# Softmax transpositions on the two row halves of TensorE, and layers 0 and 1 by groups of eight batches, in a four-layer graph network

## The chip, the cores and the metric

The kernel runs on one core of a Trainium2 chip. The metric is device time in microseconds (us), from the start of the program on the core to its end. The engines have short names in the profile: PE is TensorE's matmuls, PEld its weight loads, DVE is VectorE, ACT ScalarE, POOL GpSimd and SP SyncE. Each has its own instruction stream and runs it in order; semaphores tie the streams together. Matmuls write to PSUM, which has eight banks of 512 float32 per partition; all else lies in SBUF.

## The reference

Input x has 32 batches of 512 nodes with 64 features; adj is one 512 x 512 matrix. Four residual layers follow each other, all in float32. Each takes `h = relu(layernorm(x))` and adds a graph layer of h to x:

```python
# layer 0: x += h @ W_self + (adj @ h) @ W_nbr + bias
# layer 1: z = h; twice: z = relu((adj @ z) @ W_i); x += z
# layer 2 (GAT): Wh = h @ W.T; e = leaky_relu(e1[:, None] + e2[None, :], 0.2)
#                att = softmax(where(adj > 0, e, NEG)); x += elu(att @ Wh)
# layer 3: gat_layer(x, g, W, b):  h = x @ W;  s = (h @ h.T) * g;  s = where(s == 0, -1e16, s)
#                return softmax(s) @ h + b
#          8 heads of width 128, leaky_relu over them, one more gat_layer of width 64 on top,
#          leaky_relu, x += result
```

Layers 2 and 3 need a softmax over 512 x 512 scores: one for each batch in layer 2 and nine for each batch in layer 3 (eight heads and the output layer).

## The kernel before

The 512 nodes of a batch are split as partition p and column block c, with P = 128 partitions and C = 4 blocks. x stays in SBUF for the whole kernel as four tiles `xs[g]` of G = 8 batches each (L70). At the start seven DMAs on ACT's queue bring x (the first group two batches at a time), one on SP's brings the adjacency, and a chain of small ones on POOL's brings the weights. `ident`, the identity that transpositions need, is made on POOL ahead of these (L58). The adjacency is copied and transposed into `adj_p` and `adj_t` (L118 to L131).

Layers 0 and 1 (L187 to L327) work on pairs of batches, so that two batches of 64 features fill 128 columns. For a pair, layer 0 transposes h on PE (`pair_transpose`, L175), multiplies by the adjacency (`neighbours`, L237: four products accumulated in one bank, then an ACT copy), and projects (`project`, L247) with block-diagonal weights. Layer 1 has product, projection, relu, product, projection. The text of the kernel arranges this as one stream of slots: slot k holds layer 0 of pair k, layer 1 of pair k - 2, the end of layer 1 of pair k - 3, and the norms of the pairs k + 2 (layer 0), k - 1 (layer 1) and k - 4 (GAT), each taken over a pair alone (class `Norm`, L199). The tile framework orders each engine's instructions beforehand, with the order of the text as priority: where an instruction isn't ready by the framework's reckoning, one from later in the text may go ahead. It also puts in the semaphore waits and hands out the buffers of each pool.

Layers 2 and 3 (from L330) are a row of units, each a softmax for two things at once (k = 0, 1): 16 `Gat` units of two batches, 128 `Heads` units of two heads of one batch, and 16 `Out` units of two batches: 160 in all. A unit has four steps, and `run` (L684) lays the steps of neighbouring units over one another in slots. In slot k come, in the text: the current unit's scores for row block r (`flow_scores`, L543: two matmuls with 64 rows, one on each row half of TensorE, each into its own bank), the transposition of step j of the unit one unit and one slot back (`transpose`, L407), its reciprocal sums at j = 1 (`recips`), the values of the slot before (`values`, L420: two matmuls with 64 output columns each), the end of an earlier unit (`end`: normalising, then y_ps of Heads or the way back into x), the preparation of the next (`prep`: g_ps of Heads, gT_ps of Out), and last the softmax of row block r on DVE and ACT (`flow_rows` and `finish_rows`: s_att, t_att, negmax, then exp into `p_att`).

`transpose(j)` takes the probabilities `p_att`, which have rows n in partitions, and produces `pt_att` with columns m in partitions: for each k four transpositions of 128 x 128 into one bank `pt_ps`, followed by one ACT copy of 512 columns (L411 to L418). PSUM in these layers: `ps_s` two buffers of two banks for scores, `ps_m` three buffers of one bank shared by everything small (pt_ps, rec_ps, y_ps, g_ps, gT_ps, hx_ps and so on), `ps_v` one bank for av. gT_ps of an Out unit holds one of the three `ps_m` buffers for four slots.

`stats` (L140) takes mean and reciprocal deviation of a whole group of eight batches; before the change only layer 3's norms use it (from `Gat.end`, in two parts of 16 columns). `norm` (L163) subtracts the mean and applies relu and scale for a pair. Its statistics come from `gat_stats`, one entry for each pair.

Of the kernel before, what the change touches and what calls it, by code (L numbers as in the profile page):

```python
# [14 lines left out]
P = 128  # L15
# [7 lines left out]
def gnn_stack_kernel(  # L23
# [34 lines left out]
    ident = const.tile([P, P], F32, name="ident")  # L58
    make_identity(nc, ident)

# [8 lines left out]
    for g in range(NG):  # L69
        xg = xpool.tile([P, G, C, F], F32, name=f"x{g}")  # L70
        step = 2 if g == 0 else G
        for k in range(0, G, step):
            nc.scalar.dma_start(
                xg[:, k : k + step],
                x[g * G + k : g * G + k + step].rearrange("b (p c) f -> p b c f", c=C),
            )
        xs.append(xg)
# [36 lines left out]

    eps = const.tile([P, 1], F32, name="eps")
# [47 lines left out]
    def norm(pool, g, j, st):  # L163
        mean, rstd = (t[:, :, :, None].to_broadcast([P, 2, C, F]) for t in st)
        h = pool.tile([P, C, 2, F], F32, name="hn")
        hv = h.rearrange("p c k f -> p k c f")
        nc.vector.tensor_tensor(hv, xs[g][:, 2 * j : 2 * j + 2], mean, OP.subtract)
        for k in range(2):
            nc.vector.scalar_tensor_tensor(
                hv[:, k], hv[:, k], 0.0, rstd[:, k], op0=OP.max, op1=OP.mult  # L170
            )
        return h
# [11 lines left out]

    gat_stats = [None] * (B // 2)  # L187
    with (
        tc.tile_pool(name="ln_a", bufs=3) as lnp,
        tc.tile_pool(name="h_a", bufs=6) as hap,  # L190
# [4 lines left out]
        def pair_of(i):  # L195
            b = 2 * i
            return xs[b // G][:, b % G : b % G + 2]

        class Norm:  # L199


            def __init__(self, i):
                self.i = i

            def a(self):
                x4 = pair_of(self.i)
                self.mean = tiny.tile([P, 2, C], F32, name="mean2", bufs=B // 2 + 6)
                nc.vector.tensor_reduce(self.mean, x4, AX.X, OP.add)
                nc.vector.tensor_scalar(self.mean, self.mean, 1.0 / F, None, op0=OP.mult)
                self.h = hap.tile([P, C, 2, F], F32, name="hn")  # L210
                self.hv = self.h.rearrange("p c k f -> p k c f")
                nc.vector.tensor_tensor(
                    self.hv, x4, self.mean[:, :, :, None].to_broadcast([P, 2, C, F]),
                    OP.subtract,
                )
                self.sq = lnp.tile([P, 2, C, F], F32, name="sq")
                nc.scalar.activation(self.sq, self.hv, AF.Square)

            def b(self):
                var = tiny.tile([P, 2, C], F32, name="var2")  # L220
                nc.vector.tensor_reduce(var, self.sq, AX.X, OP.add)
                self.std = tiny.tile([P, 2, C], F32, name="std2")
                nc.scalar.activation(self.std, var, AF.Sqrt, bias=eps, scale=1.0 / F)

            def c(self):
                self.rstd = tiny.tile([P, 2, C], F32, name="rstd2", bufs=B // 2 + 6)
                nc.vector.reciprocal(self.rstd, self.std)

            def relu(self):
                for k in range(2):  # L230
                    nc.vector.scalar_tensor_tensor(
                        self.hv[:, k], self.hv[:, k], 0.0,
                        self.rstd[:, k, :, None].to_broadcast([P, C, F]),
# [38 lines left out]
        def norms(some):  # L272
            some = [n for n in some if n is not None]
            for n in some:
                n.a()
# [485 lines left out]
```

## Time and profile before

| | us |
|---|---|
| median of 3 runs | 2917.16 (2911.72 to 2918.14) |
| the profiled execution | 2918.14 |
| its span in the profile | 2916.4 |
| layers 0 and 1, last matmul of projection po1b | ends about 261.6 |
| ACT copies of pt_ps (L418), 1280 of them | 679.3 busy, 581 ns each |
| transpositions (L413), 5120 of them | 714.5 busy, 282 ns each |
| scores (L547), 2048 matmuls of Heads | 661.2 busy |
| values (L425), 2048 matmuls of Heads | 579.0 busy |

Busy time of an engine counts the stretches in which at least one of its instructions is under way, and groups of matmuls overlap, since each starts before the one before it has left the array. So for PE the distance from start to start says what an instruction costs, and the mean length of one (282 ns for a transposition) does not. A float32 product is two matmul instructions; a transposition is one. A line of the timeline gives start, length, engine, line of the kernel, operation, output and inputs, rows*columns of the array in use, shape, and how many instructions were merged. In the rows of groups the figures after the bar are busy us, mean ns of one, and idle time of the engine just before them with what ended it. In the table by stages each row ends with the granted TensorE clock (1.00 is full), the busy share of the DMA engines and GB/s.

### The profile page before, as it was taken

The numbers are of one execution on the slowest core, as the hardware profiler recorded it, in microseconds if no ns is written. First come the engines' busy times: TensorE is split into PE (matmuls) and PEld (weight loads), VectorE is DVE, ScalarE is ACT, GpSimd is POOL, SyncE is SP. The second block draws the span as 40 slices with busy tenths as digits, with TensorE's granted clock in tenths as the row PEclk, the third lists the DMA queues.
The fourth block names the chain that finished last, engine by engine and source line by source line (L and its number), as shares of the span: only waits on it lengthen the run. The fifth ranks groups of instructions, "written<-read, shape, count | busy, mean of one in ns | idle before, by whom it ended". The sixth has DMA issues, their size and how long they took to land.

```text
span 2916.4 us, 41809 instructions
## 1 busy us (share of the span) xinstructions
PE 2813.4 (96%) x15532; PEld 1380.0 (47%) x15532; DVE 2407.5 (83%) x4870; ACT 2049.0 (70%) x4687; POOL 52.7 (2%) x49
## 2 busy tenths in 40 slices
PE   7998887899999999999999999999999999999998
PEld 4555544444444444444444444444444444444443
DVE  6665889899798988888888888888888888888884
ACT  2333767677777778777777777777777777777775
POOL 3000000000000000000000000000000000000000
PEclk9998999899999999999999999999999999999999
DMA  3000000000000000000000000000000000000000
GB/s 86 1 1 1 1 1 1 1 1 1 1 5 4 1 4 1 4 1 5 1 4 1 4 1 4 1 5 1 4 1 5 1 5 1 4 1 4 1 4 4
DMA packets 9916, 13.10 MB, mean 4 GB/s; under 512 B 1016, under 2 KB 9376, under 8 KB 9584
## 3 DMA queue, kind: packets, MB, share of 16 engines
q1 hardware_dynamic: 4752, 5.24, 0.5%
q10 hardware_dynamic: 4208, 4.19, 0.5%
q8 instruction: 122, 2.00, 0.3%
q0 software_dynamic: 752, 0.99, 0.2%
q14 instruction: 82, 0.67, 0.1%
HBM read 6.23 MB, written 4.19 MB: 4 GB/s over the span
## 4 chain that ended last, share of the span: by engine, by line
PE 88%; DVE 6%; ACT 3%; issue 1%; POOL 1%; DMA 1%; POOLq 0%; DVEq 0%; ACTq 0%
PE av L425 20%; PE pt_ps L413 20%; PE s_ps L547 19%; PE rec_ps L436 6%; PE g_ps L591 5%; PE y_ps L619 4%; PE nt_ps L240 4%; PE gT_ps L642 3%; PE nt1b_ps L240 2%; ACT p_att L401 1%; DVE s_att L536 1%; PE po L251 1%; DVE t_att L397 1%; PE wh_ps L474 1%; DVE l_att L397 1%
## 5 line engine op out<-in xcount | busy, mean ns | idle before, releaser
L401 ACT ACTIVATE p_att<-t_att,negmax 128x512 f32<-128x512 f32 x1152 | 825.3, 717 | 466.3 <-DVE negmax L397 466.2
L536 DVE TENSOR_TENSOR s_att<-s_ps,adj_p 128x1024 f32<-128x1024 f32 x576 | 703.3, 1221 | 228.6 <-PE s_ps L547 228.6
L413 PEld LDWEIGHTS pt_ps<-ident,p_att 128*128 128x128 f32 x5120 | 554.8, 142 | 492.6 <-ACT p_att L401 187.5
L418 ACT COPY pt_att<-pt_ps 128x512 f32<-128x512 f32 x1280 | 679.3, 581 | 120.7 <-PE pt_ps L413 120.5
L397 DVE CUSTOM_DVE_ANT_0 t_att<-s_att,t_att 128x512 f32<-128x512 f32 x1152 | 752.3, 687 | 13.4
L413 PE MATMUL pt_ps<-ident,p_att 128*128 128x128 f32 x5120 | 714.5, 282 | 12.6 <-ACT p_att L401 7.5
L547 PE MATMUL s_ps<-hx,g 64*128 64x512 f32 x2048 | 661.2, 625 | 2.0 <-DVE s_att L536 2.0
L425 PE MATMUL av<-pt_att,hn 128*64 128x512 f32 x2048 | 579.0, 611 | 0.0
L540 DVE TENSOR_SCALAR t_att<-s_att 128x1024 f32<-128x1024 f32 x576 | 393.1, 683 | 24.3 <-ACT pt_att L418 0.5
L547 PEld LDWEIGHTS s_ps<-hx,g 64*128 64x128 f32 x2048 | 204.8, 185 | 311.3 <-issue 121.3
L401 ACT ACTIVATION_READ_ACCUMULATOR p_att<-t_att,negmax 128x1 f32 x1152 | 216.0, 187 | 0.0
L436 PE MATMUL rec_ps<-ident,rec 128*64 128x128 f32 x2560 | 186.6, 284 | 16.9 <-DVE rec L432 10.6
L436 PEld LDWEIGHTS rec_ps<-ident,rec 128*64 128x64 f32 x2560 | 144.4, 139 | 50.6 <-issue 26.5
L624 ACT ACTIVATE cat<-y_ps,bh 128x512 f32<-128x512 f32 x256 | 159.6, 672 | 4.4 <-PE y_ps L619 4.4
L425 PEld LDWEIGHTS av<-pt_att,hn 128*64 128x64 f32 x2048 | 115.6, 135 | 76.5 <-issue 76.2
L619 PE MATMUL y_ps<-o_att,wh_sb 64*128 64x512 f32 x512 | 145.8, 641 | 1.6 <-ACT pt_att L418 0.8
L591 PE MATMUL g_ps<-hx,m 64*128 64x512 f32 x256 | 144.6, 645 | 1.0 <-ACT pt_att L418 0.9
L642 PE MATMUL gT_ps<-cat,wo_sb 128*64 128x512 f32 x512 | 131.4, 595 | 0.0
L448 DVE TENSOR_TENSOR o_att<-av,recb 128x512 f32<-128x512 f32 x160 | 108.9, 681 | 21.8 <-PE av L425 20.6
L240 PE MATMUL nt_ps<-adj_t,hn 128*128 128x512 f32 x256 | 116.5, 598 | 0.0
L397 DVE DVE_READ_ACCUMULATOR2_ANT negmax<- 128x1 f32 x1280 | 104.7, 82 | 0.0
L444 ACT COPY recb<-rec_ps 128x512 f32<-128x512 f32 x160 | 93.9, 587 | 8.8 <-PE rec_ps L436 8.8
(131 smaller groups left out, 1930.4 us busy)
## 6 DMA issues: line engine op xcount, KB each, us to landing
out_dram<-x SPq DMA_DIRECT2D x32, 128.0 KB, 1.8
x<-in_x_dram ACTq DMA_DIRECT2D x3, 1024.0 KB, 13.7
x<-in_x_dram ACTq DMA_DIRECT2D x4, 256.0 KB, 7.9
adj_raw<-in_adj_dram SPq DMA_DIRECT2D x1, 1024.0 KB, 5.3
wh_sb<-in_L_gnn_Wh_dram POOLq DMA_DIRECT2D x2, 256.0 KB, 8.0
wo_sb<-in_L_gnn_W_out_dram POOLq DMA_DIRECT2D x1, 256.0 KB, 7.9
wl<-in_L_gnn_net_params_dram POOLq DMA_DIRECT2D x4, 16.0 KB, 7.0
bias_b<-in_L_gnn_bias_dram POOLq DMA_DIRECT2D x1, 32.0 KB, 7.6
```

The costliest lines, as they stand in the source:

```text
L240: nc.tensor.matmul(p, lhsT=lhs(k), rhs=adj_t[:, k, :], start=(k == 0), stop=(k == C - 1))
L397: nc.vector.tensor_tensor_reduce(out=ns[k], in0=s[k], in1=t[k], scale=-1.0, scalar=BIG, op0=OP.add, op1=OP.min, accum_out=self.negmax[:, k ...
L401: nc.scalar.activation(self.p[:, k, r, :], ns[k], AF.Exp, bias=self.negmax[:, k, r : r + 1], scale=-1.0, accum_out=self.sum[:, k, r : r + 1],)
L413: nc.tensor.transpose(ps[:, r * P : (r + 1) * P], self.p[:, k, r, j * P : (j + 1) * P], ident,)
L418: nc.scalar.copy(pt[:, k, :], ps)
L425: nc.tensor.matmul(self.av[halves(k), :], lhsT=self.v(k, j), rhs=pt[:, k, :], start=(j == 0), stop=(j == C - 1),)
L436: nc.tensor.matmul(ps[halves(k), r * P : (r + 1) * P], lhsT=rec[:, k, r : r + 1].to_broadcast([P, F]), rhs=ident, start=True, stop=True,)
L536: nc.vector.tensor_tensor(s, ps, adj_f[:, r, None, :].to_broadcast([P, 2, N]), OP.mult)
L540: nc.vector.tensor_scalar(t, s, 0.0, FLOW_NEG, op0=OP.is_equal, op1=OP.mult)
L547: nc.tensor.matmul(u.s_ps[:, k], lhsT=g[halves(k), r * P : (r + 1) * P], rhs=x[halves(k), :], start=True, stop=True,)
L591: nc.tensor.matmul(ps, lhsT=m2[rows, 2 * i : 2 * i + 2, :].rearrange("p h f -> p (h f)"), rhs=self.x[rows, :], start=True, stop=True,)
L619: nc.tensor.matmul(ps, lhsT=wh_sb[halves(k), h, :], rhs=self.o[halves(k), :], start=True, stop=True,)
```

## The change

There are three parts to it.

The softmax's transposition is done in halves. A 128 x 128 block of `p_att` becomes two inputs of 64 rows, one on each row half of the array, each with a 64 x 64 identity, and each gives 64 columns of the output. The first half's outputs of both k go to one bank, the second half's to another, and an ACT copy for each bank puts its 512 columns into `pt_att` in runs of 64. So both copies need all 16 transpositions, and the two banks are in use together.

```diff
         def transpose(self, j):
             pt = pbuf.tile([P, 2, N], F32, name="pt_att", bufs=3)
             self.pts = getattr(self, "pts", []) + [pt]
+            ps = [ps_m.tile([P, 2, C, F], F32, name="pt_ps", tag="m") for half in range(2)]
             for k in range(2):
-                ps = ps_m.tile([P, N], F32, name="pt_ps", tag="m")
                 for r in range(C):
-                    nc.tensor.transpose(
-                        ps[:, r * P : (r + 1) * P],
-                        self.p[:, k, r, j * P : (j + 1) * P],
-                        ident,
-                    )
-                nc.scalar.copy(pt[:, k, :], ps)
+                    for half in range(2):
+                        nc.tensor.transpose(
+                            ps[half][:, k, r],
+                            self.p[halves(half), k, r, j * P : (j + 1) * P],
+                            ident[halves(half), halves(half)],
+                        )
+            pth = pt.rearrange("p k (r half q) -> p k r half q", r=C, half=2)
+            for half in range(2):
+                nc.scalar.copy(pth[:, :, :, half, :], ps[half])
```

Layers 0 and 1 no longer run as a stream of slots. The class `Norm`, `norms`, `make`, `ends` and the loop over slots go; a loop over the four groups takes their place. In it, the group's statistics are taken at once, then all four norms, then the bias, then layer 0 of the four pairs, statistics again, layer 1 of each pair from norm to the final add, and statistics for the GAT. The transposed h of layer 0 is copied by DVE where ACT did it. `gat_stats` has one entry for each group.

```diff
+        for g in range(NG):
+            xg = xs[g]
+            st = stats(lambda shape: lnp.tile(shape, F32, name="sq"), G * C, g)
+            hs = [norm(hap, g, j, st) for j in range(G // 2)]
+            nc.gpsimd.tensor_tensor(
+                xg.rearrange("p b c f -> p (b c) f"),
+                xg.rearrange("p b c f -> p (b c) f"),
+                bias0_b[:, None, :].to_broadcast([P, G * C, F]),
+                OP.add,
+            )
+            for j, h in enumerate(hs):
                 ht = pair_transpose(
+                    ps_t, lambda n: wk.tile([P, N], F32, name=n), h, "ht0", nc.vector.tensor_copy
+                )
+                nt = neighbours(lambda k: h[:, k], "nt0")
+                po = project([(ht, ws2), (nt, wn2)], "po0")
+                for b in range(2):
+                    nc.vector.tensor_tensor(
+                        xg[:, 2 * j + b], xg[:, 2 * j + b], po[:, :, b, :], OP.add
+                    )
+            st = stats(lambda shape: lnp.tile(shape, F32, name="sq"), G * C, g)
+            for j in range(G // 2):
+                h = norm(hap, g, j, st)
+                nt = neighbours(lambda k: h[:, k], "nt1")
+                for i, w in enumerate(wl2):
+                    po = project([(nt, w)], f"po1_{i}")
+                    if i < len(wl2) - 1:
+                        z = wk.tile([P, C, F2], F32, name="z")
+                        nc.scalar.activation(z, po.rearrange("p c b f -> p c (b f)"), AF.Relu)
+                        nt = neighbours(lambda k: z[:, k, :], "nt1")
+                for b in range(2):
+                    nc.vector.scalar_tensor_tensor(
+                        xg[:, 2 * j + b], po[:, :, b, :], 0.0, xg[:, 2 * j + b],
+                        op0=OP.max, op1=OP.add,
+                    )
+            gat_stats.append(stats(lambda shape: lnp.tile(shape, F32, name="sq"), G * C, g))
```

The pools of these layers become `ln_a` with two buffers (three before, but of a quarter of the size) and `h_a` with `G // 2 + 2` = 6 as before. `norm` subtracts the mean batch by batch, two instructions of 256 elements where one of 512 stood, and takes its statistics as columns of the group's.

The start changes too: x comes in four DMAs of eight batches, even groups on ACT's queue and odd ones on SP's, and the identity is made after the weights' DMA issues on POOL.

```diff
-        step = 2 if g == 0 else G
-        for k in range(0, G, step):
-            nc.scalar.dma_start(
-                xg[:, k : k + step],
-                x[g * G + k : g * G + k + step].rearrange("b (p c) f -> p b c f", c=C),
-            )
+        eng = nc.scalar if g % 2 == 0 else nc.sync
+        eng.dma_start(xg, x[g * G : (g + 1) * G].rearrange("b (p c) f -> p b c f", c=C))
...
+    ident = const.tile([P, P], F32, name="ident")
+    make_identity(nc, ident)
     eps = const.tile([P, 1], F32, name="eps")
```

## The prediction

> **What bounds the kernel now.** I read the busy shares first, then the same by stage, then the order of TensorE's work inside one slot, then the rows of what changes. The page begins:
>
> ```profile
> span 2916.4 us, 41809 instructions
> ## 1 busy us (share of the span) xinstructions
> PE 2813.4 (96%) x15532; PEld 1380.0 (47%) x15532; DVE 2407.5 (83%) x4870; ACT 2049.0 (70%) x4687; POOL 52.7 (2%) x49
> ```
>
> TensorE (PE) fills 96%, VectorE (DVE) is not far behind. By stages (length, then busy us of PE, PEld, DVE, ACT, POOL, then the granted clock):
>
> ```profile
> 20.00:260.00 240.00, 231.78 (x953) 137.85 (x953) 146.44 (x336) 83.14 (x170) 18.89 (x15) 1.00 0.02 4
> 260.00:300.00 40.00, 30.42 (x124) 22.45 (x124) 29.33 (x73) 16.18 (x36) 0.00 (x0) 0.57 0.00 1
> 300.00:600.00 300.00, 250.17 (x1475) 142.89 (x1472) 267.53 (x595) 210.76 (x481) 13.70 (x6) 0.91 0.00 1
> 600.00:2800.00 2200.00, 2193.07 (x12406) 1026.93 (x12405) 1880.46 (x3701) 1661.65 (x3835) 4.57 (x2) 1.00 0.01 3
> ```
>
> Layers 0 and 1 run to about 262 us with PE never free from 27 us on. The GAT stage (to about 600) has PE at 83% and DVE at 89%: there PE is not the limit. Layer 3 (600 to 2800) is purely PE: 2193 of 2200, with DVE at 85.5% and ACT at 75.5%. In it one slot looks so in PE's timeline (start, length, operation):
>
> ```profile
> 1214.53 1.13 PE L619 MATMUL y_ps<-o_att,wh_sb 64*128 64x512 f32 x4
> 1215.49 1.02 PE L547 MATMUL s_ps<-hx,g 64*128 64x512 f32 x4
> 1216.45 1.09 PE L413 MATMUL pt_ps<-ident,p_att 128*128 128x128 f32 x8
> 1217.47 1.08 PE L425 MATMUL av<-pt_att,gV 128*64 128x512 f32 x4
> 1218.48 1.13 PE L547 MATMUL s_ps<-hx,g 64*128 64x512 f32 x4
> 1219.54 0.66 PE L413 MATMUL pt_ps<-ident,p_att 128*128 128x128 f32 x4
> ```
>
> From start to start: scores 0.96 after another 64-row operation (y_ps) but 1.06 after av, so a change of the array's form costs about 0.10 on entry; transpositions 1.02 for eight; values 1.01. The scores are four passes of 512 columns in 0.96, where the full-array neighbour products of layers 0 and 1 need 3.44 us for eight such passes in the chain of waits (0.43 each, so 1.72 for four): the two row halves do run side by side. A 64-row transposition exists once in this kernel, on one half:
>
> ```profile
> L354 PEld LDWEIGHTS whT_ps<-ident,wh_sb x8: 134/138/140, 262.5 to 262.9; 64*128 64x128 f32 x8
> L354 PE MATMUL whT_ps<-ident,wh_sb x8: 221/222/243, 262.5 to 262.9; 64*128 64x64 f32 x8
> ```
>
> The timeline gives this group 0.68 us in all; less one length of 0.22 that is 0.46 for seven steps, about 0.065 each, with loads included. A full one takes (1.02 - 0.10)/8 = 0.115.
>
> **The skill.** "TensorEngine Tiling (Array Packing)", Key Properties, says that a change of tiling mode drains TensorE and that tiles otherwise load and multiply independently; the 0.10 above and the side-by-side scores agree. Its Gotcha 1 asks for different PSUM banks for different row tiles, which the change observes; no transposition here shows it. "TensorE: Matmul & The Clock Gate", section on LDWEIGHTS, says that a load costs by columns, not rows: 138 ns with 64 rows against 140 with 128 here. Twice as many loads must therefore run in pairs to be free. Its Part 1 says that some 3.4 us of idleness halve the clock: the 0.57 at 260 to 300, where PE waits for the GAT's first rows, agrees.
>
> **Part 1, the transpositions.** Each slot issues 16 loads and 16 matmuls of 64 columns in place of 8 and 8 of 128. Side by side: 8 pairs x 0.065 = 0.52, plus 0.10 for leaving the form, 0.62 in place of 1.02. As the scores before it have the same 64-row form, the 0.10 between them goes too. Saved: 0.50 a slot. Layer 3 has 128 Heads and 16 Out units of 4 slots; the page has 5120 transpositions, 8 a slot, so 640 slots, 64 of them the GAT's. The window of 2200 us has 4380/8 = 548 slots: 274 us of PE time. What is late next is DVE: its 1880 us stay, and PE would need 2193 - 274 = 1919. Two engines with nearly the same load don't meet without loss: DVE's reciprocal waits 66.8 us for ACT's sums in this window even now, and 1880 + 67 = 1947 is a floor for DVE. The evacuations stay two ACT copies of 0.58, but both now wait for all 16 halves, where the first used to start after four transpositions; and both banks of the three in the shared PSUM pool must be free before the first transposition. Queued behind such a wait on PE are values, y_ps and the next scores, and DVE waits for those. One y_ps comes one values block (1.01) after the transpositions, while two copies need 0.2 + 1.16, so 0.3 to 0.5 us may be lost per unit, 137 units, 40 to 70 us if nothing absorbs it. I take 2020 for the window: a gain of 180. Best 1947 (253 gained), poorest about 2150 (50). Elsewhere (28 slots of layer 3, and the GAT, where DVE is the limit) 5. The copy's output in runs of 64 elements moves the same 512 elements; I cost it at nothing, 0.05 x 1280 = 64 us of ACT at worst, which has 24% free.
>
> **Part 2, layers 0 and 1.** PE's own work is the same: transpositions, three neighbour products and the projections of 16 pairs. What changes is what it waits for. A set of statistics is now taken for 8 batches at once: from the rows
>
> ```profile
> L154 POOL TENSOR_TENSOR sq<-sq 128x1024 f32<-128x1024 f32 x8 | 18.3, 2301 | 396.4 <-DVE sq L151 396.4
> L155 DVE TENSOR_REDUCE var<-sq 128x16 f32<-128x1024 f32 x8 | 9.8, 1220 | 9.7 <-POOL sq L154 9.7
> L151 DVE TENSOR_TENSOR sq<-x,mean 128x1024 f32<-128x1024 f32 x8 | 9.4, 1220 | 0.0
> L145 DVE TENSOR_REDUCE mean<-x 128x32 f32<-128x2048 f32 x4 | 9.1, 2280 | 0.0
> ```
>
> twice the length each where 1024 stands: 2.28 + 0.17 + 2.44 + 4.6 (GpSimd) + 2.44 + 0.32 + 0.34 = 12.6, some 13 with handovers. Between layers 0 and 1 of a group lie the adds (1.0), this 13 and a norm (4 x 0.415 = 1.7): 15.7 us. Between groups, serially, two statistics: 28.7. Within layer 1 a pair runs product, copy, projection, relu, product, copy, projection with three gaps of about 0.9, and the next norm may stand behind this pair's adds: 5.6 per pair; in layer 0 one gap, 0.9. With no overlap a group loses 15.7 + 28.7 + 22.4 + 3.6 = 70, four groups 280.
>
> But the engines' orders aren't the order of the text. The trace of before shows the builder filling waits with later work:
>
> ```profile
> 13.66 1.21 DVE L343 TENSOR_SCALAR neg<-adj_p 128x2048 f32<-128x2048 f32 x1
> ...
> 31.42 0.38 PE L251 MATMUL po<-ws,ht 128*128 128x128 f32 x2
> ...
> 31.64 0.60 PE L178 MATMUL ht_ps<-ident,hn 128*128 128x128 f32 x4
> ...
> 32.26 0.49 PE L251 MATMUL po<-wn,nt 128*128 128x128 f32 x2
> ```
>
> L343 stands after both layers in the text, yet runs at 13.66; and PE, stopped in a projection, takes the next pair's transpositions. So layer 0 of group g+1 (4 x 5.7 = 22.8 of PE) can cover the 15.7 before layer 1 of group g; six h tiles and two sq tiles allow about that. The last group has nothing behind it: 15.7, plus 2 for the GAT statistics of the group before in DVE's queue. Start: the first statistics (x's first megabyte in one transfer beside the adjacency's, the identity behind POOL's DMA issues, which end at 18.4) 3. The last GAT statistics, 7.5 of DVE, beside the GAT's preparation: 8. A cold clock after the wait: 4. An order fixed beforehand that takes GpSimd for faster than it is (in the GAT's statistics DVE waits 9.7 us for L154) stalls 12 statistics by about 2: 24. Sum 57; I take 60, between 20 and 280. Moving DMAs to SP's queue puts two transfers behind the adjacency there; at 20 us all are in.
>
> **The sum**, against the profiled span of 2916.4 (its run took 2918.14, the median is 2917.16): -180 - 5 + 60 = -125, so 2791; the median is 1 us beside it. I say 2790.
>
> **Rivals.**
> 1. Layers 0 and 1 lose their overlap (slower). Place: PE before L240 of layer 1, waiting for DVE's norm; price 200 to 280; with 185 gained, slower once layers 0 and 1 end later than 262 + 185 = 447 us. For: all of a group's adds precede any of its next norms, and h tiles taken by a later group can block. Against: the filling shown above. 2916 - 185 + 230 = 2961.
> 2. The halves take turns. 16 x 0.065 + 0.10 = 1.14, less the 0.10 before: no gain, and the 60 of part 2 stays: 2976. For: no transposition on two halves is in the trace. Against: scores, y_ps. Were each turn to cost a change of form (0.10), a slot would lose 0.6 and the kernel some 350; I give that 2 in 100.
> 3. DVE, ACT and the three PSUM buffers take nearly all: 60 gained, 60 lost, 2916. For: DVE at 85.5% in order; against: PE waits for a buffer almost nowhere now.
>
> **How the numbers follow.** Forecast 0.58, rival 1 0.20, rival 2 0.12, rival 3 0.10. The forecast's own range is 2690 to 2880 (best 253 gained and 20 lost: 2683; poorest 100 gained, 65 lost). The range that holds 8 in 10 reaches from 2690 to 2980, as the two slower cases hold a third. A run tells 0.2%, some 6 us, from no change: faster 0.62 (forecast 0.57, rival 3 0.04, rival 1 0.01), same 0.04, slower 0.34.
>
> **What would show it.** Right: in layer 3 the transpositions' block shrinks to about 0.62 with starts in pairs a few ns apart, DVE over 90% busy, PE waiting for s_att and pt_att; layer 3 some 180 us shorter; layers 0 and 1 ending near 320 us with gaps of PE at the last group. Wrong: a block of over 1 us (rival 2), layers 0 and 1 ending past 450 us with PE idle 15 us at each statistics (rival 1), or a block of 0.62 in a layer 3 that stays near 2200 (rival 3).

## The result, and the profile after

The changed kernel takes 3201.45 us (median of 4, 3199.8 to 3202.94) beside 2917.65 us: ratio 1.0977, 95% interval 1.0958 to 1.0996. It is slower by about 284 us, where a gain of 127 was forecast. The page of the changed kernel, the span, the busy shares and the engines of the chain that ended last:

```profile
span 3200.1 us, 51783 instructions
...
PE 2642.8 (83%) x20652; PEld 1339.2 (42%) x20652; DVE 2432.6 (76%) x4802; ACT 2002.8 (63%) x4586; POOL 99.0 (3%) x49
...
DVE 48%; PE 27%; ACT 20%; issue 4%; POOL 1%; DMA 0%; POOLq 0%; DVEq 0%; ACTq 0%
```

PE's busy time is 170 us less and DVE's and ACT's hardly changed, so no engine sets the time by its work alone any more. The chain runs through DVE for 48% and PE for 27%; before it was PE 88%, DVE 6%. The engines wait for each other. By stages (columns as in the prediction's table), first the set-up with layers 0 and 1, then 1500 us out of layer 3:

```profile
0.00:450.90 450.90, 269.19 (x978) 148.31 (x978) 180.85 (x283) 42.51 (x76) 77.54 (x40) 0.84 0.05 14
...
1000.00:2500.00 1500.00, 1324.11 (x11086) 649.34 (x11082) 1234.20 (x2439) 1093.84 (x2530) 0.00 (x0) 1.00 0.01 3
```

The same 1500 us before:

```profile
1000.00:2500.00 1500.00, 1497.52 (x8473) 700.30 (x8472) 1277.28 (x2518) 1131.26 (x2612) 0.00 (x0) 1.00 0.01 3
```

The 978 matmuls of the set-up and layers 0 and 1 are the same, but the first matmul behind them (whT_ps), which I take as their end from here on, starts at 451.0 instead of 262.5 us: +188.5. The GAT, from there to the 17th copy of rec_ps, takes 342.5 instead of 333.1: +9.4. The rest takes 2406.6 instead of 2320.8: +85.8. These add up to the 283.7 by which the spans differ. In layer 3 I use one measure from here on, the unit: the mean distance between copies of rec_ps into SBUF, of which each unit makes one, over units 21 to 151. It goes from 16.00 to 16.60 us.

**The transpositions themselves did what was forecast.** PE's timeline over some slots of layer 3, after:

```profile
1514.84 1.30 PE L476 MATMUL s_ps<-hx,g 64*128 64x512 f32 x4
1515.70 0.22 PE L340 MATMUL pt_ps<-ident,p_att 64*128 64x64 f32 x1
1516.72 0.71 PE L340 MATMUL pt_ps<-ident,p_att 64*128 64x64 f32 x15 [0.58 <-ACT cat L553]
...
1518.37 1.13 PE L476 MATMUL s_ps<-hx,g 64*128 64x512 f32 x4
1519.33 0.66 PE L340 MATMUL pt_ps<-ident,p_att 64*128 64x64 f32 x16
1519.92 1.08 PE L354 MATMUL av<-pt_att,hn 128*64 128x512 f32 x4
```

In the undisturbed slot below, 16 halves take 1519.92 - 1519.33 = 0.59, and start 0.96 after the scores. In the slot above one of the 16 goes, and the second, which needs the other bank, waits till ACT has emptied it (cat, the copy that reads y_ps).

**But DVE now stands still in the same unit.** DVE's timeline, after:

```profile
1515.78 0.08 DVE L322 DVE_READ_ACCUMULATOR2_ANT negmax<- 128x1 f32 x1
1517.98 0.20 DVE L361 RECIPROCAL rec<-sum_att 128x8 f32<-128x8 f32 x1 [2.12 <-ACT p_att L326]
1518.10 1.17 DVE L465 TENSOR_TENSOR s_att<-s_ps,adj_p 128x1024 f32<-128x1024 f32 x1
```

and before, at the same place in most of its units:

```profile
1216.57 1.23 DVE L536 TENSOR_TENSOR s_att<-s_ps,adj_p 128x1024 f32<-128x1024 f32 x1 [0.57 <-PE s_ps L547]
1218.12 0.20 DVE L432 RECIPROCAL rec<-sum_att 128x8 f32<-128x8 f32 x1 [0.33 <-ACT p_att L401]
```

The instruction of 0.20 us, the reciprocal of the softmax's sums, has changed places with the multiplication of the scores. It needs the sum of ACT's last exp. Before, a multiplication of 1.23 us ran in that time and 0.33 was left to wait; now the multiplication stands behind it, though its scores are there by 1516.14 (1514.84 + 1.30), and DVE is idle for 2.12. What ACT does meanwhile, after:

```profile
1516.00 1.25 ACT L553 ACTIVATE cat<-y_ps,bh 128x512 f32<-128x512 f32 x2
1517.14 0.71 ACT L326 ACTIVATE p_att<-t_att,negmax 128x512 f32<-128x512 f32 x1
```

The last exp begins at 1517.14, behind the two cat copies. In sums over the same 1500 us (engine, tile, line, what it waited for, us in total, times, longest), after:

```profile
DVE rec L361 <- ACT p_att L326: 169.7, 80, 2.1
...
PE g_ps L520 <- ACT pt_att L347: 89.4, 80, 1.2
...
PE pt_ps L340 <- ACT pt_att L347: 43.3, 70, 0.7
PE pt_ps L340 <- ACT cat L553: 37.8, 70, 0.9
```

and before:

```profile
DVE rec L432 <- ACT p_att L401: 46.9, 83, 2.1
...
PE gV_ps L651 <- ACT gT L648: 2.5, 11, 0.2
```

Before, the 2.5 us for gV were PE's only wait in that window. After, PE waits 175.8 us, and all but 5.3 of that is for one of the three `ps_m` banks: pt_ps takes two, rec_ps takes the third, and g_ps, next in PE's order, finds none free. The longest wait of 2.1 in the first row of before tells one thing more: in 15 units of the kernel before the reciprocal already stood in front of the multiplication and waited 2.1 us. After, 124 units have that order.

**Layers 0 and 1.** PE's waits from 20 to 460 us, after:

```profile
PE ht_ps L178 <- DVE hn L168: 64.5, 4, 21.0
...
PE nt_ps L195 <- DVE hn L168: 60.5, 4, 15.1
```

and the timeline between the first and the second group:

```profile
121.32 1.16 PE L206 MATMUL po<-wl,nt 128*128 128x128 f32 x8 [0.73 <-ACT nt L199]
...
123.31 4.48 DVE L140 TENSOR_REDUCE mean<-x 128x32 f32<-128x2048 f32 x2
...
143.53 1.11 PE L178 MATMUL ht_ps<-ident,hn 128*128 128x128 f32 x4 [21.05 <-DVE hn L168]
```

There are four gaps of 15.1 before layer 1 and three of 21.0 between groups, about 125 us in all, and nothing fills them. The two means at 123.31 say why: one is the GAT's of group 0, the other that of layer 0 of group 1. The x that the second needs is sent for at the start and takes 19.4 us to land; it could have been taken long before, but stands behind group 0's last add. The other 63 us have three parts. PE's own busy time grew from 238.0 to 269.2, with the same matmuls at a granted clock of 0.84 (1.00 before). PE waits for ACT's copies of nt and z (16.2 and 11.0, about 3 before). And at the start PE waits 25.3 for the identity on POOL.

### The profile page after: what moved, and what is told of

The parts are those of the page before. It is cut to its first block, busy times and chain, and to the rows that moved or that the text cites. A ratio compares the mean times of both kernels' runs of the same rounds, so it can differ in the third digit from the quotient of the medians.

```text
span 3200.1 us, 51783 instructions
## 1 busy us (share of the span) xinstructions
PE 2642.8 (83%) x20652; PEld 1339.2 (42%) x20652; DVE 2432.6 (76%) x4802; ACT 2002.8 (63%) x4586; POOL 99.0 (3%) x49
## 4 chain that ended last, share of the span: by engine, by line
DVE 48%; PE 27%; ACT 20%; issue 4%; POOL 1%; DMA 0%; POOLq 0%; DVEq 0%; ACTq 0%
DVE s_att L465 15%; DVE t_att L322 12%; ACT p_att L326 12%; DVE t_att L469 9%; PE nt_ps L195 6%; PE s_ps L476 4%; ACT cat L553 4%; PE g_ps L520 3%; PE av L354 3%; PE gT_ps L571 3%; DVE o_att L377 2%; ACT pt_att L347 2%; PE po L206 2%; PE pt_ps L340 2%; DVE hn L164 1%
## 5 line engine op out<-in xcount | busy, mean ns | idle before, releaser
L340 PE MATMUL pt_ps<-ident,p_att 64*128 64x64 f32 x10240 | 588.2, 228 | 165.8 <-ACT pt_att L347 74.5
L340 PEld LDWEIGHTS pt_ps<-ident,p_att 64*128 64x128 f32 x10240 | 486.9, 139 | 551.0 <-issue 181.1
L476 PE MATMUL s_ps<-hx,g 64*128 64x512 f32 x2048 | 704.6, 625 | 6.5 <-DVE s_att L465 6.5
L476 PEld LDWEIGHTS s_ps<-hx,g 64*128 64x128 f32 x2048 | 240.8, 186 | 286.4 <-issue 73.2
L361 DVE RECIPROCAL rec<-sum_att 128x8 f32<-128x8 f32 x160 | 32.2, 201 | 266.8 <-ACT p_att L326 266.8
L548 PE MATMUL y_ps<-o_att,wh_sb 64*128 64x512 f32 x512 | 193.9, 643 | 0.9 <-DVE o_att L377 0.9
L195 PE MATMUL nt_ps<-adj_t,hn 128*128 128x512 f32 x256 | 134.3, 666 | 60.5 <-DVE hn L168 60.5
L199 ACT COPY nt<-nt_ps 128x512 f32<-128x512 f32 x48 | 28.1, 586 | 237.1 <-PE nt_ps L195 237.1
L365 PEld LDWEIGHTS rec_ps<-ident,rec 128*64 128x64 f32 x2560 | 142.0, 139 | 37.8 <-ACT pt_att L347 14.9
L520 PEld LDWEIGHTS g_ps<-hx,m 64*128 64x128 f32 x256 | 37.7, 184 | 253.0 <-ACT pt_att L347 250.7
L246 DVE SCALAR_TENSOR_TENSOR x<-po,x 128x256 f32<-128x256 f32 x32 | 12.1, 419 | 167.3 <-PE po L206 167.3
## 6 DMA issues: line engine op xcount, KB each, us to landing
x<-in_x_dram SPq DMA_DIRECT2D x2, 1024.0 KB, 19.4
```

Of the source, the lines that this page charges most:

```text
L195: nc.tensor.matmul(p, lhsT=lhs(k), rhs=adj_t[:, k, :], start=(k == 0), stop=(k == C - 1))
L340: nc.tensor.transpose(ps[half][:, k, r], self.p[halves(half), k, r, j * P : (j + 1) * P], ident[halves(half), halves(half)],)
L365: nc.tensor.matmul(ps[halves(k), r * P : (r + 1) * P], lhsT=rec[:, k, r : r + 1].to_broadcast([P, F]), rhs=ident, start=True, stop=True,)
L476: nc.tensor.matmul(u.s_ps[:, k], lhsT=g[halves(k), r * P : (r + 1) * P], rhs=x[halves(k), :], start=True, stop=True,)
L520: nc.tensor.matmul(ps, lhsT=m2[rows, 2 * i : 2 * i + 2, :].rearrange("p h f -> p (h f)"), rhs=self.x[rows, :], start=True, stop=True,)
```

## The experiments

The ratio is to the kernel before, measured beside it on the same chip, with its 95% interval. The fourth column is where layers 0 and 1 end, the last the unit, both as defined above.

| kernel | median, us | ratio | layers 0, 1 | unit, us |
|---|---|---|---|---|
| before | 2912.72 to 2917.65 | 1 | 262.5 | 16.00 |
| changed | 3201.45 | 1.0977 (1.0958 to 1.0996) | 451.0 | 16.60 |
| `split_only` | 3004.19 | 1.0311 (1.0281 to 1.0340) | 262.9 | 16.60 |
| `groups_only` | 3113.20 | 1.0685 (1.0654 to 1.0716) | 448.9 | 16.00 |
| `groups_tags` | 3006.96 | 1.0320 (1.0290 to 1.0350) | 348.4 | 16.00 |
| `split_recpool` | 2870.56 | 0.9852 (0.9823 to 0.9880) | 263.4 | 15.57 |
| `before_recpool` | 2919.97 | 1.0012 (1.0002 to 1.0022) | 262.7 | 16.00 |
| `recpool_j3` | 2905.32 | 0.9963 (0.9953 to 0.9974) | 262.5 | 15.81 |
| `recpool_m4` | 2801.17 | 0.9602 (0.9575 to 0.9630) | 262.2 | 15.12 |
| `split_rec3` | 2957.29 | 1.0138 (1.0108 to 1.0167) | 262.9 | 16.29 |
| `rec_late` | 2974.10 | 1.0196 (1.0160 to 1.0233) | 263.1 | 16.34 |
| `split_m4` | 2934.59 | 1.0071 (1.0048 to 1.0094) | 263.0 | 16.08 |
| `rec_late_m4` | 2856.06 | 0.9792 (0.9763 to 0.9820) | 262.2 | 15.52 |
| `before_m4` | 2958.67 | 1.0144 (1.0084 to 1.0203) | 262.8 | 16.26 |
| `rec_two` | 2951.11 | 1.0126 (1.0094 to 1.0158) | 262.5 | 16.10 |
| `rec_two_m4` | 2966.96 | 1.0181 (1.0149 to 1.0213) | 262.2 | 16.26 |
| `rec_mid` | 2860.38 | 0.9812 (0.9773 to 0.9850) | 261.8 | 15.53 |
| `rec_mid_m4` | 2789.88 | 0.9570 (0.9533 to 0.9607) | 262.5 | 15.09 |

### Each half of the change alone

`split_only` is the kernel before with the new `transpose`; `groups_only` is the changed kernel with the old one:

```diff
-            ps = [ps_m.tile([P, 2, C, F], F32, name="pt_ps", tag="m") for half in range(2)]
             for k in range(2):
+                ps = ps_m.tile([P, N], F32, name="pt_ps", tag="m")
...
+                nc.scalar.copy(pt[:, k, :], ps)
```

> The kernel before with the halved transpositions alone; layers 0 and 1 as before. Theory: of the 284 us, about 190 belong to layers 0 and 1 (they end at 451 us instead of 262) and about 95 to the softmax layers, where the block of transpositions is short but the waits around it cost more. Then this run takes about 3010 us, layers 0 and 1 end at about 262, and a unit of layer 3 takes 16.6 us against 16.0. Rival: the halves do gain as forecast, and the softmax layers were only harmed by what the groups left behind; then about 2730 us.

> The changed kernel with the old transpositions of 128 rows. Theory (the two parts add up): about 3105 us, layers 0 and 1 end at about 451, layer 3 at 16.0 us a unit. Rival (the parts hinder each other): less than 3060 or more than 3150.

Alone, the halves cost 91.5 us and the groups 200.5; the sum of 292 is near the 284 measured together. So there are two separate faults, and each can be looked at without the other: `split_only` has the unit of the changed kernel and the waits of its layer 3 (rec 171.9, g_ps 89.3), `groups_only` its layers 0 and 1.

### Layers 0 and 1: whose buffers are they?

If it is the buffers that keep a group's statistics in the order of the text, then names (and with them buffers) of their own for each phase let the next group go ahead:

```diff
-    def stats(sq_tile, width, g):
+    def stats(sq_tile, width, g, ph="f"):
...
-        mean = tiny.tile([P, nb], F32, name="mean", bufs=NG + 1)
+        mean = tiny.tile([P, nb], F32, name="mean" + ph, bufs=2 if ph in "ab" else NG)
...
-            st = stats(lambda shape: lnp.tile(shape, F32, name="sq"), G * C, g)
-            hs = [norm(hap, g, j, st) for j in range(G // 2)]
+            st = stats(lambda shape: lnp.tile(shape, F32, name="sqa", bufs=1), G * C, g, "a")
+            hs = [norm(hap, g, j, st, "hn0") for j in range(G // 2)]
```

The same goes for var, std, rstd, for the tiles of layer 1 (`hn1`), and for the two PSUM pools, which become two buffers for each layer instead of four for both.

> As groups_only, but layer 0, layer 1 and each of the three statistics have tile names (and PSUM buffers, two and two) of their own. Theory: buffers of one name are given out in the order of the text, so the first statistics of the next group, whose mean tile stands behind the GAT mean of this group, couldn't go ahead; with names apart group g+1 covers the waits of group g, layers 0 and 1 end at 280 to 330 us, and the whole takes 2930 to 2990 us. Rival: the statistics over eight batches and the chains are long in themselves; then layers 0 and 1 still end past 420 us and the whole takes about 3090.

Layers 0 and 1 end at 348.4 instead of 448.9: names and buffers, with the same instructions, give back 100 us of the 186. So tiles of their own are worth more than half of the loss; the expectation was still missed (by 18 us at the end of the layers and by 17 in the whole). The edit changes numbers too: h tiles go from 6 to 12 and squares from 2 to 3, so how much is the order and how much the number of buffers wasn't separated. For the mean that stood behind group 0's last add the number was not it: it was the fourth mean, and `mean` had five buffers. The first 348 us of `groups_tags`:

```profile
0.00:348.30 348.30, 253.82 (x978) 142.89 (x978) 195.93 (x283) 42.30 (x76) 70.99 (x40) 0.93 0.07 18
```

PE still waits 17.8 and 15.3 at the start (identity, adj_t), 11.8 and twice about 6.2 later and 18.6 at the last group, behind which there is no other; the clock is 0.93. How much of these 86 us a better order could still win wasn't tried.

### Layer 3: the reciprocal off DVE

If DVE loses by standing at the reciprocal, then it must help to do that on an engine that has nothing else to do. `split_recpool` is `split_only` with the reciprocal as a power of -1 on POOL (`self.one` holds -1.0); `before_recpool` does the same to the kernel before:

```diff
-            nc.vector.reciprocal(rec, self.sum)
+            nc.gpsimd.tensor_tensor(rec, self.sum, self.one, OP.pow)
```

> As split_only, but the reciprocal of the sums is taken by GpSimd (a power of -1) and no longer by VectorE. Theory: in the changed kernel VectorE waits 2.1 us in each unit at this reciprocal for ScalarE's last exponential, with the next scores' multiplication queued behind it; with the wait moved to an idle engine a unit takes 14.3 to 15.3 us and the whole 2690 to 2830 us. Rival: the three PSUM buffers, held until ScalarE has copied both halves, set the pace; then the unit stays above 16.2 us and the whole above 2950.

> The kernel before (transpositions of 128 rows, layers 0 and 1 as a stream) with the reciprocal of the sums on GpSimd as a power of -1. Theory: before, TensorE sets the pace, so taking VectorE's wait at the reciprocal away changes nothing: 2905 to 2920 us. Rival: that wait cost time before as well, and the gain of split_recpool over split_only is nothing that the halves have to do with; then 2850 us or less.

One small instruction on another engine is worth 134 us of `split_only`'s 3004, and the halves now beat the kernel before by 1.5%. The time lies between what the theory gave (2690 to 2830) and what the rival gave (above 2950), so this is not all. In the kernel before, where PE sets the pace, the same edit brings nothing. PE's waits for g_ps in the 1500 us fall from 89.3 to 55.4, and its waits for pt_ps behind pt_att from 43.4 to 3.8.

It remained possible that the benefit was POOL's and not that of DVE's order. Four kernels keep the reciprocal on DVE. `split_rec3` only calls it later, at j == 3:

```diff
-                if j == 1:
+                if j == 3:
                     u.recips()
```

> As split_only (reciprocal on VectorE), with recips called at step 3. The reciprocal stays at the same place in VectorE's order, one place before a multiplication of scores, but ScalarE's order changes: the cat copies no longer stand between the last exponentials. If VectorE's wait came from those copies, it falls from 2.1 us to under 1 us a unit and the run takes 2800 to 2930 us; if the place in VectorE's order alone makes it, it stays near 3000.

The wait stays (173.8 in the 1500 us), so this says nothing of its cost. The expectation had the mechanism wrong: the cat copies still stand between the last two exps in ACT's order (exp at 1501.00, cat at 1501.72, exp at 1502.86), and the reciprocal still waits 2.12. The 47 us gained come from elsewhere: g_ps, which waited 89.3 in `split_only`, no longer finds the banks full. That this is what they come from isn't shown; the same move costs time in `recpool_j3` below.

`rec_late` ties the reciprocal behind the multiplication, by adding zero times four elements of each half of that s_att to the sums:

```diff
+            src = self.sum
+            if Pair.s is not None:
+                nc.vector.scalar_tensor_tensor(
+                    rec, Pair.s[:, :, :C], 0.0, self.sum, op0=OP.mult, op1=OP.add
+                )
+                src = rec
+            nc.vector.reciprocal(rec, src)
```

> As split_only, but the reciprocal on VectorE reads eight elements of the current s_att (times zero) and so stands behind the multiplication of scores, a slot later; one small instruction more for each unit. If its place in VectorE's order is what costs, VectorE's wait for ScalarE's sums at it disappears and the time is that of split_recpool, 2850 to 2890 us. If GpSimd itself made the gain, or the sums are late anyway, it stays above 2950.

DVE's wait goes, and another takes its place on PE, which needs `rec` for rec_ps:

```profile
PE rec_ps L447 <- ACT p_att L402: 114.1, 81, 2.0
```

It names ACT, but ACT's sums had been there for some time; what came late was the reciprocal behind the multiplication. In one unit of its trace the addition that reads the sums starts at 1504.34, the reciprocal at 1506.23 and rec_ps at 1506.58. Of the 134 us only 30 are won. So in `rec_two` the reciprocal stays at j == 1 and rec_ps is made one slot later (`spread` at j == 2), and in `rec_mid` both are one step earlier, so that PE's order is that of `split_only` and only DVE's differs (the two traces show PE's and ACT's instructions of layer 3 in the same order; DVE has one small instruction more a unit):

```diff
-                if j == 1:
+                if j == 0:
                     u.recips()
+                if j == 1:
+                    u.spread()
```

> As rec_late, but the broadcast of the reciprocals on TensorE (rec_ps) is called at step 2, a slot after the reciprocal on VectorE. In rec_late the wait only changed sides: TensorE waited 1.4 us a unit at rec_ps. If a wait for ScalarE's sums at a place with something queued behind it is what costs, neither VectorE nor TensorE waits at the reciprocal now, and the time falls from 2974 to 2850 to 2900 us, as with GpSimd. If the sums aren't the cause, it stays above 2950.

> As rec_two, each part called one step earlier: the reciprocal on VectorE stands one multiplication of scores later than in split_only, where it stands in the kernel before, and TensorE's order is that of split_only. Theory: with the order of the other engines kept, taking VectorE's wait away is worth about what GpSimd's reciprocal was, 1.0 us a unit: 2850 to 2900 us, with no wait at rec on VectorE and under 0.3 us a unit at rec_ps on TensorE. If it is worth half of that or less (2930 us or more), the rest of GpSimd's gain is its relief of VectorE and the order that came with it.

`rec_two` missed: neither DVE nor PE waits for rec any more, but rec_ps now falls into the slot of y_ps, and pt_ps waits for cat (71.7) and y_ps for pt_att (23.7). Those are waits for the three banks again; that they make the loss isn't shown, since with a fourth bank (`rec_two_m4` below) they go and the time doesn't fall. `rec_mid` settles the question of DVE's order. Its waits:

```profile
DVE s_att L552 <- PE s_ps L563: 142.9, 180, 4.4
...
DVE rec L439 <- ACT p_att L402: 0.2, 1, 0.2
```

With the reciprocal on DVE, behind the multiplication as in the kernel before, the time is 2860, as with POOL or a little less (0.9773 to 0.9850 beside 0.9823 to 0.9880; the intervals overlap). So the gain doesn't need POOL. Against `split_only` the place of this one instruction is worth 144 us, 1.07 a unit. It is not the whole wait of 171.9: with it gone DVE waits 142.9 for scores, where it waited 68.9.

### Layer 3: the three banks

The other suspect is `ps_m`. `recpool_j3` moves rec_ps out of the crowded slot. The kernels with `_m4` free one bank for `ps_m`: the scores get three buffers of one bank each instead of two of two, and their multiplication goes in two instructions of 512:

```diff
-    ps_s = ctx.enter_context(tc.tile_pool(name="ps_s", bufs=2, space=PSUM))
-    ps_m = ctx.enter_context(tc.tile_pool(name="ps_m", bufs=3, space=PSUM))
+    ps_s = ctx.enter_context(tc.tile_pool(name="ps_s", bufs=3, space=PSUM))
+    ps_m = ctx.enter_context(tc.tile_pool(name="ps_m", bufs=4, space=PSUM))
...
-        nc.vector.tensor_tensor(
-            s, ps, adj_f[:, r, None, :].to_broadcast([P, 2, N]), OP.mult
-        )
+        for k in range(2):
+            nc.vector.tensor_tensor(s[:, k], ps[k], adj_f[:, r], OP.mult)
```

> As split_recpool, with the whole of recips called at step 3 of the transpositions, two slots later. rec_ps then doesn't share a slot with g_ps. Theory: what is left in layer 3 is TensorE waiting for one of three PSUM buffers, most at g_ps behind two transposition banks and rec_ps; without rec_ps there, g_ps waits less and a unit gains 0.3 to 0.8 us: 2740 to 2830 us in all. Rival: VectorE and ScalarE are the limit, or the wait moves to the slot that gets rec_ps; then 2855 to 2885.

> As split_recpool, with scores in three banks of one k each in place of two pairs, their multiplication by the adjacency as two instructions of 512, and a fourth buffer in the shared PSUM pool. If the three shared buffers are the limit: TensorE's waits at g_ps and pt_ps fall below a third of split_recpool's, and the time falls under 2830 us, unless the narrower room for scores takes it back, which would show as VectorE waiting for s_ps longer than before. If they aren't: 2860 us or more with those waits gone.

`recpool_j3` missed: g_ps's wait goes as expected, but pt_ps waits more for cat (56.3 after 36.0), y_ps and the way back to x begin to wait (7.8 and 6.9), and the unit grows by 0.24. With three banks, moving a user moves the wait. Why the unit grows isn't shown, for PE's waits in sum fall from 100.6 to 80.1. With the fourth bank, `recpool_m4`, the waits of g_ps and pt_ps are gone and the time falls by a further 69 us. Then av heads PE's list, waiting 54.8 us for DVE's o_att to free the only av bank. The `_m4` edit also makes the scores' buffers and multiplication finer; what of its worth is that and what the bank wasn't separated.

Is the fourth bank worth the same when DVE still waits? And does it alone help the kernel before?

> As split_only with three single banks for scores and four shared PSUM buffers; the reciprocal stays on VectorE, before a multiplication of scores. If the two waits are separate costs, the buffers are worth here what they were beside split_recpool (70 us, 0.45 us a unit): 2920 to 2950 us, with VectorE's wait at the reciprocal still 1.5 to 2 us a unit. If they are one loop, in which the late copies made the sums late, the wait falls too and the time is under 2870.

> Halved transpositions, stream of slots, the late reciprocal on VectorE and four shared PSUM buffers. If both causes are found, this is as fast as recpool_m4 or a little faster: 2770 to 2815 us, with VectorE busy over 90% of layer 3. If not, 2850 or more.

> The kernel before with the single-bank scores and four shared PSUM buffers, transpositions of 128 rows. Theory: before, TensorE sets the pace and waits for no buffer, so this is no faster: 2910 to 2990 us (VectorE has 576 instructions more, and the reciprocal comes to stand before a multiplication of scores). Rival: buffers were short before too; then under 2890.

`split_m4` is 70 us below `split_only` with the wait for rec still at 128.4: here the bank and the reciprocal are two costs that add up. `rec_late_m4` missed its 2770 to 2815: it gains 118 over `rec_late`, but PE still waits for rec_ps, 117.8. `before_m4` is slower by 1.4%, though PE waits only 2.7 us (gV) and is busy for 1491.75 of the 1500 us: here too the order has flipped, and rec waits 128.2. So the flip doesn't belong to the halves; the `_m4` edit alone brings it about. That the flip is why this kernel is slower is not shown: DVE isn't its limit, and why PE fills more time with the same instructions stays open.

> As rec_two, with three single banks for scores and four shared PSUM buffers. Both waits gone without GpSimd: 2770 to 2830 us, VectorE over 90% busy in layer 3. If GpSimd did more than take a wait away, it stays above 2850.

> As rec_mid, with three single banks for scores and four shared PSUM buffers. If buffers and reciprocal are separate costs: 60 to 80 us less than rec_mid, 2780 to 2830 us. If the two touch the same time, within 40 us of rec_mid.

`rec_mid_m4` is the best of all, 4.3% under the kernel before. The middle of its layer 3:

```profile
1000.00:2500.00 1500.00, 1432.31 (x12176) 730.22 (x12174) 1383.18 (x3177) 1190.99 (x2779) 0.00 (x0) 1.00 0.01 3
```

DVE is busy for 92%, PE for 95%; PE's chief wait is av for o_att, 55.7. `rec_two_m4` missed, and by much: with the same edit on `rec_two` the kernel became slower, not faster. In the 1500 us its av waits 142.9 us in all, up to 2.2 at a time, for o_att, and its clock isn't full; the row of waits, and the first 500 us:

```profile
PE av L430 <- DVE o_att L463: 142.9, 83, 2.2
...
1000.00:1500.00 500.00, 453.27 (x3760) 223.53 (x3758) 430.34 (x982) 371.99 (x857) 0.00 (x0) 0.95 0.01 3
```

By the trace's record of the clock 133 of the 1500 us ran at half clock. If PE had set the pace throughout, that would cost 67 us, by my estimate 0.7 a unit; so the clock may be a large part of the miss, but no run separates it from the waits. With this run and `before_m4`, the fourth bank is no gain everywhere.

## Why the prediction was wrong

**Part 1, PE's own work: right.** "8 pairs x 0.065 = 0.52, plus 0.10 for leaving the form" gave a block of 0.62; it is 0.59. The 0.10 between scores and transpositions is gone as well (0.96 in place of 1.06). From scores to values it is 0.96 + 0.59 = 1.55 after 1.06 + 1.02 = 2.08: 0.53 saved a slot, where 0.50 was forecast. Rival 2, the halves taking turns, is out.

Four smaller readings of this part were off. The 0.10 was read as a cost "on entry" alone; it is paid at either end (last section), which the sum had right. A change of form at each of 16 turns would have cost 1.6 a slot, not the 0.6 of rival 2's working; no other number rests on that. DVE, forecast to be over 90% busy, is at 82% (1234 of 1500 us). And of what the prediction takes from the page on loads, its trace agrees on the rows alone: in the kernel before, loads of 128 rows have records of 140 ns with 128 columns (pt_ps) and 136 with 64 (av), so a cost by columns doesn't show in their length.

**Part 1, "DVE's reciprocal waits 66.8 us ... 1880 + 67 = 1947 is a floor": this step failed.** It took a wait seen before as a constant, and took DVE's order as given. Nor was that wait one small delay in every unit: about 32 of the 66.8 us came from the 15 units of before whose order was already the bad one, 2.1 each. The orders are made anew for every kernel, and in the new one the reciprocal stands before the multiplication that used to cover its wait. In the 1500 us the wait is 1.88 a unit (169.7 by 1500/16.60 units) after 0.50 (46.9 by 1500/16.00); what its place costs, by `rec_mid` against `split_only`, is 1.07 a unit. The page showed what was needed to see the danger: DVE works in order, a small instruction depended on ACT's last exp, all that hid it was one multiplication of 1.23 us in front of it, and the longest wait of 2.1 showed units without that cover. What makes the builder choose the one order or the other, I don't know; that it chose so is in the trace, and that the choice costs this much is shown.

**Part 1, the banks, "40 to 70 us if nothing absorbs it": the term was put in the wrong place; its size fits.** The forecast priced a wait at y_ps, and its 2020 leaves 73 us above the floor of 1947 for it. It came at g_ps, behind rec_ps, and at pt_ps: 1.89 us a unit of PE waiting (89.4 + 43.3 + 37.8 by 90.4 units). The fourth bank, with the finer scores that it needs, brings about 70 us (`recpool_m4`, `split_m4`, `rec_mid_m4`), at the upper end of the range given. The rest of that waiting is presumably time that PE would have lost to DVE anyway; that isn't shown. So the sum had room for the banks, and what broke it in layer 3 is the reciprocal's place and an unexplained rest. "TensorEngine Tiling (Array Packing)", section PSUM Bottleneck, says that tiling speeds up TensorE but not the emptying of PSUM; the trace agrees: ACT's copies still take 580 ns each (581 before), and a slot's transpositions now need two banks at once.

Unit by unit: 180 us by 137 units meant 16.00 - 1.31 = 14.69. Measured is 16.60. Of the 1.91 between, 1.07 is the reciprocal's place (16.60 to 15.53), 0.44 the fourth bank, with the multiplication in two parts that it needs (15.53 to 15.09), and 0.40 is left. As the 14.69 had room for the banks already (73 by 137, or 0.53), some 0.9 is unexplained. DVE in `rec_mid_m4` has 13.9 us of work a unit (1383 of 1500 by 15.09), so DVE's work alone doesn't rule out the 14.69; the parts of the rest weren't separated and stay open.

**Part 2, "layer 0 of group g+1 ... can cover the 15.7": this step failed too.** Layers 0 and 1 make the larger part of the loss, 188.5 of 284 us. Of the forecast's error they make the smaller: 128 (188.5 where 60 was forecast), while layer 3 went from -180 to +86, an error of 266. The gaps were sized well (15.1 measured for 15.7) and placed as in the serial case; that they'd be filled was argued from before's timeline, where later work does fill waits. But work can be drawn forward only if its buffers can be. In before the norms of layer 0 stood in the text two pairs ahead of their use; in the changed text layer 0's statistics of group g+1 use the same names as the GAT's of group g and stand behind them. The working counted the buffers ("six h tiles and two sq tiles allow about that") and left out the order in which they are given out. `groups_tags` shows that names and buffers of their own bring 100 us back; that it is the order is shown for the mean alone. The serial sum of 280 was too high: the waits within the pairs, 104 of it (four times 22.4 + 3.6), came to 27 (16.2 + 11.0), and between groups there were three gaps of 21.0 for four of 28.7. "A cold clock after the wait: 4" was too low: PE's busy time grew by 31 us, at a mean clock of 0.84. "TensorE: Matmul & The Clock Gate", Part 1, says that an idle window of about 3.4 us halves the clock, and seven gaps of 15 to 21 us agree: the clock is 0.60 from 120 to 150 us, where one of them lies, and 1.00 from 90 to 120, where there is none. The 3 for the start was some 8.

**Elsewhere, -5 for the GAT:** it is +9.4.

**The rivals.** Rival 1 had half of the place (60.5 of the 125 us lie before layer 1, the rest before the next group's layer 0), nearly the price (188, a little under its 200 to 280) and the point right: layers 0 and 1 end at 451, past its 447. It missed the time (2961) because it too credited layer 3 with the gain. Rival 3 had the right suspects for layer 3 and the wrong size for them: it left layers 2 and 3 a gain of 60 us, which became a loss of 95. Its sign, a block of about 0.6 in a layer 3 that gets no shorter, and rival 1's, an end past 450 us with gaps of 15, came true together.

## What to carry to other kernels

Where engines work in order, look for small instructions that wait for another engine and ask what stands before them now and what would stand there after the change: a cover of one instruction is luck, not a constant. A row of waits whose sum is far below its count times its longest may hold two cases, as here, so look at both. A faster operation that holds two buffers of a pool of three can be paid for by the pool's other users, so try it with a buffer more (four kernels here gained 69 to 118 us by that, two became slower), and check PE's waits by tile. And before counting on work from later in the text to fill a gap, see whether its tiles share a name with the work it must pass.

## What the runs showed of the hardware

Sixteen half transpositions on two row halves and two banks take 0.59 us, the pairs about 62 ns apart and the two of a pair 2 to 7 ns, as against eight full ones in 1.02. Each change of the array's form costs 0.10, going in and coming out: from the start of four score matmuls to that of the transpositions behind them it is 0.86 with no change on either side (1514.84 to 1515.70, after), 0.96 with one (1518.37 to 1519.33, after) and 1.06 with two (1218.48 to 1219.54, before).

The clock can be lost without long pauses. In `rec_two_m4` PE is 91% busy and waits at most 2.2 us at a time, yet the granted clock is 0.95; in the changed kernel, with 88% and waits up to 1.2, it is 1.00, though its waits come to more in sum (175.8 us after 142.9 in the 1500). "TensorE: Matmul & The Clock Gate", under A second HAM failure mode, tells of frequent short pauses that make the clock swing, and `rec_two_m4` agrees. The traces show which pause does it. Their record of the clock holds 1.0 and 0.5 alone, and it changes only on a grid of 3.41 us. In the 1500 us of `rec_two_m4`, `rec_late` and `rec_late_m4` there are 106 waits of PE of over 1.5 us, most of them about 1.9. Of the 55 that lie within one step of that grid, 51 are followed by a step at half clock; of the 51 that lie across a border of it, one is. These are 52 of the 56 steps at half clock. So less than the idle window of 3.4 us named above is enough: here some 1.9 us, when they fall into one step.
